# The second gate's logits of the first three units: from transposes and products on TensorE to multiply-and-sum passes on VectorE

## The chip, the core and the metric

The kernel runs on one core of a Trainium2 chip. A core has five engines that run side by side, each through its own list of instructions in order: TensorE (PE in the profile, with its weight loads as PEld), VectorE (DVE), ScalarE (ACT), GpSimd (POOL) and SyncE (SP), which here only issues DMA transfers. On-chip data lies in SBUF (128 partitions); products land in PSUM, from which VectorE or ScalarE has to take them. An engine waits at an instruction until what it needs is signalled by a semaphore, and all behind it on that engine waits too. The metric is the device time of one execution, in microseconds (us).

## What is computed

Eight batches of 256 tokens of width 128 go through two layers, each a conditioning step followed by a mixture of eight experts. Cut to the part that the change touches, the second layer is:

```python
def _L1_ffn_ref(x, gate_w, w1, b1, w2, b2, gamma, beta):
    residual = x
    mu = jnp.mean(x, axis=-1, keepdims=True)
    var = jnp.mean(jnp.square(x - mu), axis=-1, keepdims=True)
    xn = (x - mu) * jax.lax.rsqrt(var + LN_EPS) * gamma + beta
    probs = jax.nn.softmax(jnp.einsum('bld,de->ble', xn, gate_w), axis=-1)
    w, idx = jax.lax.top_k(probs, TOP_K)
    w = w / jnp.sum(w, axis=-1, keepdims=True)
    ...
    h = jax.nn.gelu(jnp.einsum('bld,edh->eblh', xn, w1) + b1[:, None, None, :], approximate=False)
    out_e = jnp.einsum('eblh,ehd->ebld', h, w2) + b2[:, None, None, :]
    output = jnp.einsum('ble,ebld->bld', cw, out_e)
    return output + residual
```

Here E is 8 experts, H 512 and TOP_K 2. The logits of the second gate are the `einsum('bld,de->ble', xn, gate_w)`: for each token the sum over 128 features of normalized x, times gamma, plus beta, times the gate's column. In the first layer every expert works on every token; in the second only the two best experts of each token do.

## The kernel before

**Tiling.** The 2048 tokens are five units: units 0, 1 and 2 have 4 tiles of 128 tokens (512), units 3 and 4 have 2 (256). `GT` is 4, so `nt == GT` picks units 0 to 2.

**The first layer** (`layer`) goes over units and, in each, over the 8 experts. For an expert, TensorE makes four hidden products (hp, L931), ScalarE takes each through the activation into hT (L933), and one expert later TensorE makes four products into an output yp (L911). VectorE multiplies yp by the gate's row (part_first, L899; that frees one of two PSUM buffers of yp) and adds it to the unit's sum (acc_first, L901). The gate rows come by a DMA of SyncE each time (gbc, L891). In float32 a product is two passes of TensorE, so a profile counts 320 for 160.

**What runs in between.** After each TensorE product `layer` calls `pump()`, which takes one step of a generator at the head of a queue, `behind`. In that queue lie, one after the other, the first layer's pooling, the search for its threshold (`threshold`, whose counting passes are L521, fl), and then, each appended when a unit's sum is ready, `adapt(u)`. So the work of a unit's `adapt` is spread between the products of the next unit, and each `adapt` begins only when the one before it has ended. A `yield` in a generator gives one product's time to the others.

**`adapt(u)`** adds the sum to x (x2T, L682; x, L686 from transposes fp, L556), runs the conditioning step (adp, L693; ha, L695; dp, L703), normalizes twice (`normed`: bn_stats L565, L566, rstd on GpSimd L572, L577), which gives zn, the first part of zr, and then makes the second gate's logits: for units 0 to 2 it transposes zn (znp, L737), takes it to SBUF with gamma and beta applied (znT, L742), multiplies by the gate on four column groups (l1q, L751), takes that down (l1s, L754), transposes it back (l1p, L758) and copies the logits to lg (L766). The short units do the same with plain products (l1p, L763). Then `top_one` picks the best expert (mx, s, ms, oh, L591 to L598), again for the second (rest, L770), th and a ScalarE tanh give the two weights (L776, L777), and sofar (L790) holds the running picks. TensorE's kp (L796, L797) counts, over tokens, how many picks of each expert came before; from it VectorE makes each token's row (pos, L816), and GpSimd scatters the tokens to DRAM (xs, L818), 8 scatters for a unit of 512. For units 2, 3 and 4 VectorE then writes the list of the tiles that are full (L638 to L674, `tiles_of`, `cumulated`, `listed`).

**The second layer** goes over 36 and a few more tiles of 128 rows: SyncE fetches the rows and the expert's weights by register offsets (L962, L970), VectorE multiplies the expert's row of b2all by the token's weight (b, L1003), TensorE transposes the rows (xtp, L991), VectorE takes them down with gamma and beta (xc, L993), then come hidden products (hps, L1006), activations (hs, L1008), output products (yps, L1015) and yt (L1019). The first three tiles are begun inside the first layer's last unit. The table b2all (128 partitions, 8 x 128) is loaded once, at the start, from a DRAM copy of b2 (L616, L619).

**The order** of each engine's list is fixed when the program is built; only the beginning and the ending are put in order by hand, in between a scheduler places the instructions, and they may stand in another order than in the source. `CHAIN_GAP`, 5, is the number of steps that `adapt` of a long unit lets pass between zn and its transposes.

Of the kernel before, what the change touches and what calls it, by code (L numbers as in the profile page):

```python
# [10 lines left out]
F32 = mybir.dt.float32  # L11
# [47 lines left out]
CHAIN_GAP = 5  # L59
# [10 lines left out]
C_G1 = C_G0 + E  # L70
# [4 lines left out]
C_LG = C_B21 + E  # L75
C_LB = C_LG + 1
# [12 lines left out]
def tile_adaln_ffn_d2(ctx: ExitStack, tc: tile.TileContext, x, ptype, lang, cols, b1v,  # L89
                      w10, w20, w11d, w21d, lw1, lw2, lgb, out):  # L90
    nc = tc.nc
# [419 lines left out]
    def threshold():  # L511
        lflat = logit.rearrange("p e t -> p (e t)")

        def below(values, name):

            n = values.shape[1]
            c = small.tile([P, 3], BF16, tag="kc", name=f"kc_{name}")
            for i in range(n):
                flags = small.tile([P, P], BF16, tag="flags", name=f"fl_{name}_{i}", bufs=2)
                with nc.allow_low_precision("counts up to 128, which bf16 holds exactly"):  # L520
                    nc.vector.tensor_scalar(flags, lflat, values[:, i:i + 1], None, ALU.is_lt, ALU.add,  # L521
                                            accum_out=c[:, i:i + 1])
            tot = pss.tile([P, 3], F32, tag="sm", name=f"kt_{name}")
            nc.tensor.matmul(tot[:, :n], lhsT=one16, rhs=c[:, :n], start=True, stop=True)  # L524
            return tot[:, :n]

        tot = below(steps.bitcast(F32)[:, SEARCH, 0:1], "s")
        found = small.tile([P, 1], I32, tag="found", name="found_s")
        nc.vector.tensor_scalar(found, tot, float(KTH), -1.0, ALU.is_gt, ALU.mult)
        for k, low in enumerate((*range(29, 0, -2), 0)):  # L530

            n = 3 if low else 1
            trial = small.tile([P, 3], I32, tag="tr", name=f"tr_{low}")[:, :n]
            nc.vector.tensor_scalar(trial, steps[:, k, :n], found, None, ALU.bitwise_xor)
            for _ in range(SEARCH_GAP if k else 0):
                yield
            tot = below(trial.bitcast(F32), str(low))
            ok = small.tile([P, 3], F32, tag="ok", name=f"ok_{low}")[:, :n]
            up = small.tile([P, 1], F32, tag="up", name=f"up_{low}")
            nc.vector.tensor_scalar(ok, tot, float(KTH), None, ALU.is_le, ALU.add, accum_out=up)  # L540
            bits = small.tile([P, 1], I32, tag="bits", name=f"bits_{low}")
            nc.vector.tensor_scalar(bits, up, float(1 << low), None, ALU.mult)
            after = small.tile([P, 1], I32, tag="found", name=f"found_{low}")
            nc.vector.tensor_tensor(after, found, bits, ALU.bitwise_xor)
            found = after
        gate = const.tile([P, P], F32, name="gate")
        nc.vector.scalar_tensor_tensor(gate, lflat, found.bitcast(F32), lflat, ALU.is_ge, ALU.mult)
        yield
        yield
        gd0[0] = rows_to_dram(gate, P, "L0")  # L550
# [57 lines left out]
    holding = const.tile([P, E], F32, name="holding")  # L608

    b2d = dram.tile([E, P], F32, name="b2d")  # L610
    b2all = const.tile([P, E, D], F32, name="b2all")
    w21 = const.tile([P, E, HC * D], F32, name="w21")


# [1 line left out]
    nc.sync.dma_start(out=b2d, in_=b2r)  # L616
    for e in range(E):
        nc.sync.dma_start(out=w21[:, e, :], in_=w21d[e].rearrange("p c d -> p (c d)"))
    nc.sync.dma_start(out=b2all.rearrange("p e d -> p (e d)"),  # L619
                      in_=b2d.rearrange("e d -> (e d)").partition_broadcast(P))  # L620
    for n in range(EARLY, B):
        nc.sync.dma_start(out=ys[n * 4 * P:(n + 1) * 4 * P, :].rearrange("(p t) d -> p t d", t=GT), in_=empty[:, :, :D])
    rows = xs.rearrange("(p m t) c -> p m (t c)", p=P, t=GT)
# [53 lines left out]
    def adapt(u, acc):  # L677
        g, o, nt = UNITS[u]
# [51 lines left out]
            nc.scalar.copy(zr[1][:, :, :D], zn)  # L730
        for s in range(2):
            nc.gpsimd.tensor_copy(zr[s].bitcast(I32)[:, :, D], dest[:, s, t0:t0 + nt])
        for _ in range(CHAIN_GAP if nt == GT else not last_unit):
            yield
        zp = psb.tile([P, GT, P], F32, tag="big", name=f"znp{u}")[:, :nt, :]
        for t in range(nt):
            nc.tensor.transpose(zp[:, t, :], zn[:, t, :], ident)  # L737
        if nt == GT:
            zt = keep.tile([P, GN], F32, tag="poolT", name=f"znT{u}")
        else:  # L740
            zt = work.tile([P, n], F32, tag="znT", name=f"znT{u}", bufs=1)
        nc.vector.tensor_scalar(zt, zp.rearrange("p t d -> p (t d)"), col[:, C_LG:C_LG + 1],  # L742
                                col[:, C_LB:C_LB + 1], ALU.mult, ALU.add)
        yield
        if not last_unit:
            yield
        if nt == GT:

            lq = pss.tile([P, P], F32, tag="sm", name=f"l1q{u}")
            for t in range(nt):  # L750
                nc.tensor.matmul(lq[t * A:(t + 1) * A, :], lhsT=col[:, C_G1:C_G1 + A], rhs=zt[:, t * P:(t + 1) * P],  # L751
                                 start=True, stop=True)
            ls = work.tile([P, P], F32, tag="gT", name=f"l1s{u}")
            nc.vector.tensor_copy(ls, lq)  # L754
            yield
            yield
            lp = pss.tile([P, GT, A], F32, tag="sm", name=f"l1p{u}")
            nc.tensor.transpose(lp.rearrange("p t c -> p (t c)"), ls, ident)  # L758
            lp = lp[:, :, :E]
        else:  # L760
# [4 lines left out]
        lg = small.tile([P, GT, E], F32, tag="ex", name=f"lg{u}")[:, :nt, :]  # L765
        nc.vector.tensor_copy(lg, lp)  # L766
# [92 lines left out]
    def run(key, steps):  # L859
        yield from steps  # L860
        done.add(key)
# [136 lines left out]
    def hidden(k, xt, wt, xc):  # L998
        hp = psb.tile([P, HC, P], F32, tag="big", name=f"hps{k}")
        hT = work.tile([P, HC, P], F32, tag="scr", name=f"hs{k}", bufs=NSCR)  # L1000

        b2 = work.tile([P, GN], F32, tag="gbc", name=f"b2_{k}", bufs=4)[:, :D]
        nc.vector.tensor_tensor(b2, b2all[:, bass.ds(number(k, DVE), 1), :].rearrange("p o d -> p (o d)"),  # L1003
                                xt[:, D + 1:D + 2].to_broadcast([P, D]), ALU.mult)
        for c in range(HC):
            nc.tensor.matmul(hp[:, c, :], lhsT=wt[:, c * P:(c + 1) * P], rhs=xc, start=True, stop=True)  # L1006
        for c in range(HC):
            nc.scalar.activation(hT[:, c, :], hp[:, c, :], AF.Gelu, bias=b1all[:, bass.ds(number(k, ACT), 1), c])  # L1008
        return k, xt, hT, b2
# [93 lines left out]
    def early():  # L1103
        for k in range(LEAD + PRIMED):
            ahead(k)
        for _ in range(PRIMED):
            flipped.append(turn(*fetched.popleft()))

    behind.append(run("poolings", poolings()))
    behind.append(run("threshold", threshold()))  # L1110
    layer("first", AF.Gelu_apprx_tanh, poolT, w10s, w20s, C_B10, C_B20, gates0, "pool", adapt,
          early)

# [101 lines left out]
```

## Time and profile before

| what | us |
|---|---|
| median of 5 runs | 354.61 (354.21 to 356.51) |
| profiled execution: its time | 357.72 |
| profiled execution: span from the first to the last instruction | 356.0 |
| TensorE's granted clock, mean, of full speed | 0.985 |
| first layer's products L931 and L911, busy | 119.9 and 119.6 |
| VectorE, all second-gate operations to be removed (L742, L754, L766 of three units) | 2.4, 0.9, 0.6 |
| weight load or product kp waiting for sofar, five times | 3.5 |

The profile is one execution, taken by the hardware's profiler. The span is divided among engines, which overlap, so busy times don't add up to it. A group's row gives the count, the busy time and the mean length of one instruction in ns, then the idle time of the engine just before and what ended it. VectorE's instructions overlap at their ends, so that two of them may start closer together than one is long. An operation with a sum beside its output shows as two rows, the operation and DVE_READ_ACCUMULATOR.

### The profile page before, as it was taken

How to read it: one execution, taken by the hardware profiler on the slowest of the kernel's cores; microseconds unless marked ns; L12 is line 12 of the kernel's file. 1: busy time of each engine (PE TensorE's matmuls, PEld its weight loads, DVE VectorE, ACT ScalarE, POOL GpSimd, SP SyncE). 2: the span in 40 equal slices, each digit the busy share in tenths (PEclk: the TensorE clock that was granted, in tenths of full speed). 3: DMA queues.
4: the chain of work that ended last, by engine and by line, in shares of the span. 5: the costliest groups of instructions: out<-in, count | busy, mean ns of one | idle time of the engine just before them, and what ended most of it. 6: DMA issues, size and time to landing. Idle time of an engine off the chain costs nothing. (4 is left out here: it accounts for less than half of the span.)

```text
span 356.0 us, 6113 instructions
## 1 busy us (share of the span) xinstructions
PE 338.8 (95%) x1668; PEld 223.4 (63%) x1668; DVE 201.0 (56%) x839; ACT 157.9 (44%) x359; POOL 93.6 (26%) x146
## 2 busy tenths in 40 slices
PE   6999999999999999999999999999999995999991
PEld 5794444444444444444444578877878995999990
DVE  2685666543144774765631267496697785345761
ACT  3476345534443335433344235443536643555620
POOL 6500000000000040452052013046143745555510
PEclk9899999999999999999999999999999999899998
DMA  5792599935223202121011012112756761677273
GB/s 169 232 343 77 146 354 381 380 135 166 74 70 111 62 29 59 52 69 29 30 63 56 15 31 37 40 45 75 193 173 191 187 175 45 158 216 222 89 253 113
DMA packets 35787, 47.56 MB, mean 134 GB/s; under 512 B 5465, under 2 KB 18604, under 8 KB 35752
## 3 DMA queue, kind: packets, MB, share of 16 engines
q1 hardware_dynamic: 32888, 42.31, 39.9%
q0 software_dynamic: 2144, 4.19, 3.4%
q10 hardware_dynamic: 720, 0.66, 0.5%
q8 instruction: 15, 0.25, 0.3%
q14 instruction: 20, 0.16, 0.2%
HBM read 32.66 MB, written 14.66 MB: 133 GB/s over the span
## 5 line engine op out<-in xcount | busy, mean ns | idle before, releaser
L933 ACT ACTIVATE hT_first<-hp_first,col 128x512 f32<-128x512 f32 (+1 forms) x160 | 92.8, 602 | 92.4 <-PE hp_first L931 82.9
L931 PE MATMUL hp_first<-poolT,w 128*128 128x512 f32 (+1 forms) x320 | 119.9, 512 | 0.6 <-ACT hT_first L933 0.6
L911 PE MATMUL yp_first<-hT_first,w 128*128 128x512 f32 (+1 forms) x320 | 119.6, 512 | 0.0
L911 PEld LDWEIGHTS yp_first<-hT_first,w 128*128 128x128 f32 x320 | 58.8, 190 | 45.3 <-issue 41.0
L931 PEld LDWEIGHTS hp_first<-poolT,w 128*128 128x128 f32 x320 | 58.5, 190 | 45.5 <-issue 40.2
L1008 ACT ACTIVATE hs<-hps,col 128x128 f32<-128x128 f32 x144 | 40.8, 369 | 38.1 <-PE hps L1006 21.5
L818 POOL DMA_INDIRECT xs<-zr,pos x32 | 31.9, 998 | 66.7 <-DVE pos L816 31.2
L1015 PE MATMUL yps<-w,hs 128*128 x288 | 38.7, 279 | 3.3 <-ACT hs L1008 3.1
L899 DVE SCALAR_TENSOR_TENSOR part_first<-yp_first,col,gbc_first 128x512 f32<-128x512 f32 (+1 forms) x28 | 17.2, 614 | 42.1 <-PE yp_first L911 40.9
L1022 POOL DMA_INDIRECT ys<-yt,xt x32 | 32.5, 1017 | 31.2 <-DVE yt L1019 24.4
L1006 PE MATMUL hps<-xc,wt 128*128 128x128 f32 x288 | 39.1, 280 | 0.5 <-issue 0.5
L1015 PEld LDWEIGHTS yps<-w,hs 128*128 128x128 f32 x288 | 35.6, 195 | 4.2 <-issue 4.2
L1006 PEld LDWEIGHTS hps<-xc,wt 128*128 128x128 f32 x288 | 35.9, 196 | 0.3 <-issue 0.2
L1019 DVE SCALAR_TENSOR_TENSOR yt<-yps,xt,b 128x128 f32<-128x128 f32 x36 | 12.5, 348 | 22.5 <-PE yps L1015 13.9
L572 POOL TENSOR_TENSOR rstd_l<-ve_l,nhalf 128x4 f32<-128x4 f32 (+1 forms) x5 | 5.2, 1040 | 68.2 <-DVE ve_l L570 67.5
L901 DVE TENSOR_TENSOR acc_first<-acc_first,part_first 128x512 f32<-128x512 f32 (+1 forms) x35 | 20.1, 580 | 0.5
L506 POOL DMA_DIRECT2D gd_L<-gT_L x1 | 0.7, 660 | 63.3 <-DVE gT_L L504 63.3
L919 ACT ACTIVATE y_first<-yp_first,col 128x512 f32<-128x512 f32 x8 | 5.5, 687 | 23.2 <-PE yp_first L911 14.6
L993 DVE TENSOR_SCALAR xc<-xtp,col 128x128 f32<-128x128 f32 x36 | 14.3, 401 | 0.0
L521 DVE TENSOR_SCALAR_CACHE_REDUCE fl<-logit,tr 128x128 bf16<-128x128 f32 x46 | 13.5, 343 | 0.6
L1003 DVE TENSOR_TENSOR b<-b2all,xt 128x128 f32<-128x128 f32 x36 | 10.2, 287 | 5.8 <-DMA xt<-xs 1.7
L540 DVE TENSOR_SCALAR_CACHE_REDUCE ok<-kt 128x3 f32<-128x3 f32 (+1 forms) x16 | 2.6, 160 | 13.8 <-PE kt L524 13.8
(241 smaller groups left out, 296.8 us busy)
## 6 DMA issues: line engine op xcount, KB each, us to landing
wt<-in_w_dram SPq DMA_DIRECT2D x36, 256.0 KB
xs<-empty SPq DMA_DIRECT2D x1, 8580.0 KB
w<-in_w_dram SPq DMA_DIRECT2D x24, 256.0 KB
gbc_first<-gd_L SPq DMA_DIRECT2D x24, 256.0 KB
xt<-xs SPq DMA_DIRECT2D x36, 65.0 KB
gbc_first<-gd_L SPq DMA_DIRECT2D x16, 128.0 KB
yg<-ys SPq DMA_DIRECT2D x8, 256.0 KB
xg<-in_x_dram SPq DMA_DIRECT2D x8, 128.0 KB
```

The lines of the kernel that those rows point to most:

```text
L521: nc.vector.tensor_scalar(flags, lflat, values[:, i:i + 1], None, ALU.is_lt, ALU.add, accum_out=c[:, i:i + 1])
L818: move = nc.gpsimd.indirect_dma_start(out=xs, out_offset=bass.IndirectOffsetOnAxis(ap=pos[:, t:t + 1], axis=0), in_=zr[s][:, t, :], in_off ...
L899: nc.vector.scalar_tensor_tensor(part, y, bias, gbc, ALU.add, ALU.mult)
L901: nc.vector.tensor_tensor(accs[u], accs[u], part, ALU.add)
L911: nc.tensor.matmul(yp, lhsT=w2s[e][:, c, :], rhs=hT[:, c, :], start=(c == 0), stop=(c == HC - 1))
L931: nc.tensor.matmul(hp, lhsT=w1s[e][:, c * P:(c + 1) * P], rhs=sources[g][:, o * P:o * P + n], start=True, stop=True)
L933: nc.scalar.activation(hT[:, c, :], hp, act, bias=col[:, cb1 + e * HC + c:cb1 + e * HC + c + 1])
L993: nc.vector.tensor_scalar(xc, tp, col[:, C_LG:C_LG + 1], col[:, C_LB:C_LB + 1], ALU.mult, ALU.add)
L1006: nc.tensor.matmul(hp[:, c, :], lhsT=wt[:, c * P:(c + 1) * P], rhs=xc, start=True, stop=True)
L1008: nc.scalar.activation(hT[:, c, :], hp[:, c, :], AF.Gelu, bias=b1all[:, bass.ds(number(k, ACT), 1), c])
L1015: nc.tensor.matmul(yp, lhsT=hT[:, c, :], rhs=w21[:, bass.ds(ek, 1), c * D:(c + 1) * D], start=(c == 0), stop=(c == HC - 1))
L1022: move = nc.gpsimd.indirect_dma_start(out=ys, out_offset=bass.IndirectOffsetOnAxis(ap=xt.bitcast(I32)[:, D:D + 1], axis=0), in_=yt, in_off ...
```

## The change

For units 0 to 2 the logits come from VectorE alone. A new generator, `second_gate`, stands in `behind` after `threshold`: it scales the identity by gamma (scale), multiplies the gate by it on TensorE, so that g1p holds the 8 x 128 table gamma times gate, and beside it, in a 129th column, beta times gate; it copies the table to SBUF (g1r), writes it to DRAM (g1d) and loads it back to all partitions (g1all, 128 x 8 x 129). `adapt` then makes, for each of 8 experts and 4 tiles, one `scalar_tensor_tensor` with constant 1, zn times the table's row, whose sum over the 128 features goes into lg: 32 passes for a unit, 96 in all, with a `yield` after every third; one addition then puts in the beta column. The transposes, products and copies of these units (L737, L742, L751, L754, L758, L766) are gone, and so is their gap of `CHAIN_GAP` steps: from zn to the logits there were 9 yields, now there are 11. The tables g1all and b2all share one buffer (`tag="eight"`, `bufs=1`), so b2all is now loaded after unit 2's logits, on SyncE's queue, where it has to wait until the last of them has read g1all. Units 3 and 4 stay as they were.

```diff
-    b2all = const.tile([P, E, D], F32, name="b2all")
+    g1d = dram.tile([E, D + 1], F32, name="g1d")
+    eights = {}
+
+    def eight(name, rows, width):
+
+        eights[name] = const.tile([P, E, D + 1], F32, tag="eight", name=f"{name}all", bufs=1)[:, :, :width]
+        nc.sync.dma_start(out=eights[name].rearrange("p e d -> p (e d)") if width > D else eights[name],
+                          in_=rows.rearrange("e d -> (e d)").partition_broadcast(P) if width > D else
+                          rows.partition_broadcast(P))
+
+    def second_gate():
+        scale = work.tile([P, P], F32, tag="gT", name="scale")
+        nc.vector.tensor_scalar(scale, ident, col[:, C_LG:C_LG + 1], None, ALU.mult)
+        yield
+        yield
+        g1p = pss.tile([E, D + 1], F32, tag="sm", name="g1p")
+        nc.tensor.matmul(g1p[:, :D], lhsT=col[:, C_G1:C_G1 + E], rhs=scale, start=True, stop=True)
+        nc.tensor.matmul(g1p[:, D:], lhsT=col[:, C_G1:C_G1 + E], rhs=col[:, C_LB:C_LB + 1], start=True, stop=True)
+        g1r = const.tile([E, D + 1], F32, name="g1r")
+        nc.vector.tensor_copy(g1r, g1p)
+        nc.sync.dma_start(out=g1d, in_=g1r)
+        eight("g1", g1d, D + 1)
...
-    nc.sync.dma_start(out=b2all.rearrange("p e d -> p (e d)"),
-                      in_=b2d.rearrange("e d -> (e d)").partition_broadcast(P))
...
-        for _ in range(CHAIN_GAP if nt == GT else not last_unit):
+        lg = small.tile([P, GT, E], F32, tag="ex", name=f"lg{u}")[:, :nt, :]
+        if nt == GT:
+
+            g1 = eights["g1"]
+            for n, (e, t) in enumerate(itertools.product(range(E), range(nt))):
+                spent = small.tile([P, D], F32, tag="spent", name=f"spent{u}_{n}", bufs=2)
+                nc.vector.scalar_tensor_tensor(spent, zn[:, t, :], 1.0, g1[:, e, :D], ALU.mult, ALU.mult,
+                                               accum_out=lg[:, t, e:e + 1])
+                if n % 3 == 2:
+                    yield
+            nc.vector.tensor_tensor(lg, lg, g1[:, :, D].unsqueeze(1).to_broadcast([P, nt, E]), ALU.add)
+            if u == NU - 3:
+                eight("b2", b2d, D)
             yield
...
-        if nt == GT:
-
-            lq = pss.tile([P, P], F32, tag="sm", name=f"l1q{u}")
-            for t in range(nt):
-                nc.tensor.matmul(lq[t * A:(t + 1) * A, :], lhsT=col[:, C_G1:C_G1 + A], rhs=zt[:, t * P:(t + 1) * P],
-                                 start=True, stop=True)
-            ls = work.tile([P, P], F32, tag="gT", name=f"l1s{u}")
-            nc.vector.tensor_copy(ls, lq)
-            yield
-            yield
-            lp = pss.tile([P, GT, A], F32, tag="sm", name=f"l1p{u}")
-            nc.tensor.transpose(lp.rearrange("p t c -> p (t c)"), ls, ident)
-            lp = lp[:, :, :E]
...
-        nc.vector.tensor_tensor(b2, b2all[:, bass.ds(number(k, DVE), 1), :].rearrange("p o d -> p (o d)"),
+        nc.vector.tensor_tensor(b2, eights["b2"][:, bass.ds(number(k, DVE), 1), :].rearrange("p o d -> p (o d)"),
...
     behind.append(run("threshold", threshold()))
+    behind.append(run("gate", second_gate()))
```

More of the change, by code (lines that the diff above doesn't have):

```diff
@@ L732, in adapt @@
             nc.gpsimd.tensor_copy(zr[s].bitcast(I32)[:, :, D], dest[:, s, t0:t0 + nt])
-        for _ in range(CHAIN_GAP if nt == GT else not last_unit):
-            yield
-        zp = psb.tile([P, GT, P], F32, tag="big", name=f"znp{u}")[:, :nt, :]
-        for t in range(nt):
-            nc.tensor.transpose(zp[:, t, :], zn[:, t, :], ident)
-        if nt == GT:
-            zt = keep.tile([P, GN], F32, tag="poolT", name=f"znT{u}")
-        else:
+        lg = small.tile([P, GT, E], F32, tag="ex", name=f"lg{u}")[:, :nt, :]
@@ new lines, in adapt @@
+        if nt == GT:
[9 more added lines that the diff above has]
+                eight("b2", b2d, D)
+            yield
+        else:
+            for _ in range(not last_unit):
+                yield
+            zp = psb.tile([P, GT, P], F32, tag="big", name=f"znp{u}")[:, :nt, :]
+            for t in range(nt):
+                nc.tensor.transpose(zp[:, t, :], zn[:, t, :], ident)
@@ L741, in adapt @@
             zt = work.tile([P, n], F32, tag="znT", name=f"znT{u}", bufs=1)
-        nc.vector.tensor_scalar(zt, zp.rearrange("p t d -> p (t d)"), col[:, C_LG:C_LG + 1],
-                                col[:, C_LB:C_LB + 1], ALU.mult, ALU.add)
-        yield
-        if not last_unit:
+            nc.vector.tensor_scalar(zt, zp.rearrange("p t d -> p (t d)"), col[:, C_LG:C_LG + 1],
+                                    col[:, C_LB:C_LB + 1], ALU.mult, ALU.add)
             yield
-        if nt == GT:
-            lq = pss.tile([P, P], F32, tag="sm", name=f"l1q{u}")
-            for t in range(nt):
-                nc.tensor.matmul(lq[t * A:(t + 1) * A, :], lhsT=col[:, C_G1:C_G1 + A], rhs=zt[:, t * P:(t + 1) * P],
-                                 start=True, stop=True)
-            ls = work.tile([P, P], F32, tag="gT", name=f"l1s{u}")
-            nc.vector.tensor_copy(ls, lq)
-            yield
-            yield
-            lp = pss.tile([P, GT, A], F32, tag="sm", name=f"l1p{u}")
-            nc.tensor.transpose(lp.rearrange("p t c -> p (t c)"), ls, ident)
-            lp = lp[:, :, :E]
-        else:
+            if not last_unit:
+                yield
@@ L764, in adapt @@
                                  start=True, stop=True)
-        lg = small.tile([P, GT, E], F32, tag="ex", name=f"lg{u}")[:, :nt, :]
-        nc.vector.tensor_copy(lg, lp)
+            nc.vector.tensor_copy(lg, lp)
         oh1, l1 = top_one(lg, f"p{u}")
```

## The prediction

> **What bounds the kernel now.** First the busy time by engine, then the same by stage, then TensorE's instructions in order of time around the removed ones. The chain of waits is of no use here: it stops after its last piece, a ScalarE copy of 0.36 us.
>
> ```profile
> PE 338.8 (95%) x1668; PEld 223.4 (63%) x1668; DVE 201.0 (56%) x839; ACT 157.9 (44%) x359; POOL 93.6 (26%) x146
> ```
>
> ```profile
> core 0: us, PE busy (x) PEld busy (x) DVE busy (x) ACT busy (x) POOL busy (x), PEclk, DMA share, GB/s
> 118.00:148.00 30.00, 29.66 (x94) 13.12 (x93) 19.75 (x73) 10.44 (x17) 5.17 (x6) 1.00 0.16 40
> 205.00:235.00 30.00, 29.94 (x154) 24.50 (x154) 19.87 (x82) 13.68 (x33) 3.77 (x5) 1.00 0.15 36
> ```
>
> These two stretches hold the routing of units 0 and 2. TensorE is busy 29.7 and 29.9 of 30 us, VectorE 19.8: TensorE's list sets the pace, and what is taken from it, or makes it wait, moves the end. VectorE has 10 us free in 30, but not at every moment.
>
> ```profile
> 137.04 0.60 PE L737 MATMUL znp<-ident,zr 128*128 128x128 f32 x4
> 137.48 1.02 PE L911 MATMUL yp_first<-hT_first,w 128*128 128x512 f32 x2
> 138.34 1.02 PE L931 MATMUL hp_first<-poolT,w 128*128 128x512 f32 x2
> 139.29 0.42 PE L751 MATMUL l1q<-znT,col 128*32 128x128 f32 x8
> 139.65 1.98 PE L931 MATMUL hp_first<-poolT,w 128*128 128x512 f32 x4
> 141.47 0.27 PE L758 MATMUL l1p<-ident,l1s 128*128 128x128 f32 x1
> 141.58 1.02 PE L931 MATMUL hp_first<-poolT,w 128*128 128x512 f32 x2
> 142.44 2.74 PE L911 MATMUL yp_first<-hT_first,w 128*128 128x512 f32 x6
> 145.52 0.19 PE L796 MATMUL kp<-sofar,one 128*128 128x40 bf16 x1 [0.34 <-DVE sofar L790]
> 145.58 1.10 PE L911 MATMUL yp_first<-hT_first,w 128*128 128x512 f32 x2
> ```
>
> Columns: start, length, engine, line, operation. The reader sees three removed pieces (znp, l1q, l1p) between expert products, and kp, which stays, and for which TensorE stands still until VectorE has finished sofar.
>
> **What is removed from TensorE.** An expert's four products of 512 columns (8 passes) start 3.43 us apart from the next ones (127.60, 131.04, 134.47), 0.429 a pass. znp costs 137.48 - 137.04 = 0.44. l1q: 138.34 plus two passes is 139.20, work goes on at 139.65: 0.45. l1p: 139.65 plus four passes is 141.37, on at 141.58: 0.21. Together 1.10; the same sums give 1.09 in unit 1 (znp at 169.16) and 1.10 in unit 2 (224.68). **Removed: 3.3.** Added once: g1p, two passes of 128 columns (0.11 each, as znp) and two of one column (l1p of the short units takes 0.37 for four narrow ones): **0.4**. Net -2.9.
>
> **What a pass on VectorE costs.** No row has this operation with a sum and two sources, so it comes from neighbours.
>
> ```profile
> 56.02 0.35 DVE L521 TENSOR_SCALAR_CACHE_REDUCE fl<-logit,tr 128x128 bf16<-128x128 f32 x1
> 56.29 0.09 DVE L521 DVE_READ_ACCUMULATOR fl<-logit,tr 128x1 bf16 x1
> 56.29 0.34 DVE L521 TENSOR_SCALAR_CACHE_REDUCE fl<-logit,tr 128x128 bf16<-128x128 f32 x1
> 56.55 0.09 DVE L521 DVE_READ_ACCUMULATOR fl<-logit,tr 128x1 bf16 x1
> ```
>
> ```profile
> L899 DVE SCALAR_TENSOR_TENSOR part_first<-yp_first,col,gbc_first 128x512 f32<-128x512 f32 x14 | 10.5, 750 | 35.6 <-PE yp_first L911 35.5
> L686 DVE TENSOR_TENSOR x<-fp,xg 128x512 f32<-128x512 f32 x3 | 2.1, 691 | 2.3 <-PE hp_first L931 1.7 <-PE fp L556 0.6
> L547 DVE SCALAR_TENSOR_TENSOR gate<-logit,found 128x128 f32<-128x128 f32 x1 | 0.4, 353 | 0.0
> ```
>
> ```profile
> L593 DVE TENSOR_TENSOR s_p<-lg,mx_p x5: 174/191/193, 142.2 to 285.0; 128x32 f32<-128x32 f32 x3, 128x16 f32<-128x16 f32 x2
> L770 DVE SCALAR_TENSOR_TENSOR rest<-oh_p,lg x5: 165/191/193, 143.1 to 286.4; 128x32 f32<-128x32 f32 x3, 128x16 f32<-128x16 f32 x2
> ```
>
> The threshold's counting passes (fl, 128x128 with a sum, a scalar from a column) follow each other every 0.265 us, the reading of the sum inside that. A column scalar costs 0.059 (L899 less L686); a constant costs nothing (L770 as L593), and the new passes have the constant 1. So 0.265 - 0.059 = 0.207. As a check: two tensor operations of 256 (L716) start 0.334 apart; less 128 elements at 1.06 ns ((688 - 417)/256, L901) leaves 0.198. Bounds: 0.20 below; above, gate's 353 ns with an unhidden 86 ns reading, 0.44. I take 0.207, as both neighbours agree.
>
> [...]
>
> VectorE gains 96 x 0.207 = 19.9 and loses 3 x (0.81 + 0.28 + 0.19) = 3.8. What matters is whether sofar comes in time for kp, behind which all expert products stand. Where an operation stands in each engine's list is read from the order of the two built programs; a "pair" is part_first and acc_first of one expert (0.78 + 0.69, or 0.93 for 256 columns), which stand among the passes.
>
> **Unit 0.** zr starts at 131.86 in both kernels, and the next operation at 132.89. In the new list come 32 passes (6.62) with one part/acc pair among them (1.5): logits at 141.0. The table's bias add 0.13, then the chain from mx to sofar, 142.00 to 145.46 = 3.46, with the next pair inside (about 1.25): 145.8. kp now stands after the first product of the next unit's expert 1: 134.47 + 3 x 3.43 + 0.86 = 145.6. **Wait 0.2.**
>
> **Unit 1.** Counted from the start of expert 1's hidden products (146.52 before): dp stands 1.4 further back in the list (8.7 for 7.3), so zr comes 18.3 after, not 16.9. Add 1.04 for zr, 1.5 + 1.5 for two pairs, 6.62, 0.25, 3.46: sofar at 32.7. kp's place, after expert 5's hidden products: 4 x 6.86 + 3.43 + 2.04 (the adapter's products) = 32.9. **No wait.**
>
> **Unit 2** runs beside 256-column products, 1.73 a group. 220.35 + 6.62 + two pairs 1.86 + 0.25 + 4.05 (229.67 to 233.72, a pair inside) = 233.1; kp's place 222.96 + 6 x 1.73 = 233.3. **No wait.** Here an output buffer is freed late too: expert 5's pair ends near 230.4, needed by expert 7 at 231.6.
>
> kp cost TensorE 0.56, 0.57 and 0.29 before (the passes around it), 1.42; now 0.2 each (as kp of unit 4, at 288.39), and 0.2 of wait: 0.8. **-0.6.** ScalarE's tanh (th) waits for VectorE too, with the next activations behind it; it is due 1.8 before sofar (143.68 for 145.46), and its activations feed products of the next expert, so it costs nothing unless VectorE is later than kp can bear anyway.
>
> **What moves.** The routing takes two steps more, so unit 3's adapter and routing come one expert later: kp3 from before expert 7's hidden products to the first of expert 6's outputs. One of the first b operations now stands before sofar is done; kp3 would wait about 0.8 (0.2 before). After it VectorE has some 18 operations (list of tiles, one pair), near 3.9 us, before the first xc, and TensorE has 1.3 + 0.2 + 1.7 until it needs that: 0.6 for 0.37 before. **+0.9**, at nothing to 2.5.
> On SyncE's queue the b2 load moves from 44.40 behind the gate rows of unit 4's expert 0. It waits for the table's last reading, near 228, and is issued near 236; a 256 KB gate load took 3.1 from issue (81.37) to use (84.50), so 512 KB are an estimated 6, before the first use at 260.8: 18 of cover; without it up to 6. Gate loads queue behind it, but VectorE reaches them later. g1's write and its 516 KB load go in among the gate loads at 81 to 89; what stands behind is first needed at 101.7, the table at 132.9. POOL's scatters follow kp, which in unit 2 keeps its time to 0.3; the first tile fetch (248.49) was 12 ahead of its transpose (262.28).
>
> **Sum.** -2.9 - 0.6 + 0.9 = -2.6. The profiled span of 356.0 (357.72 with what lies around it) becomes 353.4. The median shown, 354.61, becomes **352.0**.
>
> **Rivals.**
> *VectorE late (slower).* Each pass longer by d makes each of three waits longer by 32 d. With x = 32 d the waits are 0.2 + x, x - 0.2 and x - 0.2: the added cost is 3x - 0.4 once x passes 0.2. It eats the gain at x = 1.0 (a pass of 0.238) and makes the kernel 0.5% slower from x = 1.6 (0.257). If fl's 0.265 holds as it stands, x = 1.86, +5.2: 357.2. At gate's 353 plus 86 ns, x = 7.4: 374. For it: that row 0.265, and that no row has this form. Against: the column scalar's 0.059. Chance 0.30, for passes from 0.257 on.
> *Given back at the boundary (no change).* kp3 and the first tiles wait 2.5 rather than 0.9, and unit 0 waits up to 1 more: 353.6 to 354.6. For it: VectorE is busy for 20.1 of 27 us from 235 to 262 and takes work of unit 3 into the next stretch. Against: TensorE was idle there for less than 1 us, so the lists fit. Chance 0.15.
> *TensorE's gain doesn't reach the end*, as ScalarE or a transfer sets it: at 297.3 all engines stand still for 3.1 us until ScalarE goes on, with no cause that the trace names. If that instant is fixed: 354.6. Chance 0.05.
> Forecast: 0.50.
>
> **How the numbers follow.** The forecast's own range: no wait before kp and no cost at the boundary, -3.7, to the 0.5% below, -1.8: 350.9 to 352.8. 0.5%, 1.8 us, is about what a measurement of this kernel can tell from no change. With the others the range is **350.5 to 358.5**; above it lies a pass of 0.28 or more, 0.13, below it 0.04. Faster by more: 0.50, the forecast. Within it: 0.20, the second and third rival. Slower: 0.30, the first.
>
> **What would show it.** In the profile after: znp, l1q and l1p of three units gone from TensorE; 96 passes, each with a reading of the sum, every 0.20 to 0.22 us; TensorE's idle time before kp released by sofar, under 1 us in all; kp3 and the first hps waiting about 1.4 together; b2all landed before 250. The prediction is wrong if passes start more than 0.24 apart: then TensorE waits before kp three times, by 32 times the excess each.

## The result, and the profile after

The changed kernel took 356.9 us (353.77 to 361.82), the kernel before 355.35 (353.49 to 362.58) beside it: a ratio of **1.0034, with a 95% interval of 1.0018 to 1.005**. The ratio goes by the executions within 1.5% of the fastest of their kernel, which leaves out 7 of the 36 and 4 of the 62 that the ranges include. That is within the 0.5% that the prediction called no change, but its interval lies above 1: a little slower, where 352.0, faster, had been forecast. The profiled execution has a span of 356.2, before 356.0.

First the busy time by engine of the changed kernel's page, then the same two stretches as before.

```profile
PE 335.6 (94%) x1633; PEld 222.2 (62%) x1633; DVE 218.5 (61%) x1027; ACT 158.1 (44%) x359; POOL 93.6 (26%) x146
```

```profile
core 0: us, PE busy (x) PEld busy (x) DVE busy (x) ACT busy (x) POOL busy (x), PEclk, DMA share, GB/s
118.00:148.00 30.00, 29.93 (x83) 13.21 (x82) 25.17 (x132) 11.42 (x19) 4.05 (x5) 1.00 0.13 42
205.00:235.00 30.00, 29.36 (x143) 24.80 (x143) 25.16 (x145) 14.28 (x34) 3.78 (x5) 1.00 0.20 52
```

TensorE lost 3.2 us of work (338.8 to 335.6), and the span lost nothing: the 3.2 us became idle time. VectorE went from 19.8 to 25.2 in each stretch. In the first one TensorE is as full as it was, in the second it has begun to wait.

VectorE's instructions in order of time, in unit 0: start, length, engine, line, operation.

```profile
133.21 0.28 DVE L759 SCALAR_TENSOR_TENSOR spent<-zr,g1all 128x128 f32<-128x128 f32 x1
133.43 0.08 DVE L759 DVE_READ_ACCUMULATOR spent<-zr,g1all 128x1 f32 x1
133.43 0.28 DVE L759 SCALAR_TENSOR_TENSOR spent<-zr,g1all 128x128 f32<-128x128 f32 x1
133.64 0.08 DVE L759 DVE_READ_ACCUMULATOR spent<-zr,g1all 128x1 f32 x1
```

A pass starts every 0.2125 us; the reading of its sum lies inside. The prediction had 0.207. TensorE's list beside them (the view of the first two rows ends at 140):

```profile
134.79 3.60 PE L928 MATMUL yp_first<-hT_first,w 128*128 128x512 f32 x8
138.22 2.31 PE L948 MATMUL hp_first<-poolT,w 128*128 128x512 f32 x5
...
141.66 3.60 PE L928 MATMUL yp_first<-hT_first,w 128*128 128x512 f32 x8
145.09 1.02 PE L948 MATMUL hp_first<-poolT,w 128*128 128x512 f32 x2
146.18 0.18 PE L813 MATMUL kp<-sofar,one 128*128 128x40 bf16 x1
```

Groups of four products follow one another every 3.43 with nothing in between: znp, l1q and l1p are gone. Two passes from 145.09 would end at 145.95; kp starts at 146.18, a wait of 0.2, as forecast. The gain is really made here. Next, where it goes: all waits of TensorE over 0.5 us between unit 1's routing and unit 4's adapter, with what stands on the releasing engine. (kp0 to kp3 and dp3 are kp and dp of that unit.)

```profile
179.39 0.18 PE L813 MATMUL kp<-sofar,one 128*128 128x40 bf16 x1 [0.84 <-DVE sofar L807]
...
229.59 0.20 ACT L794 ACTIVATE th<-th 128x4 f32<-128x4 f32 x1 [2.96 <-DVE th L793]
230.21 0.70 PE L948 MATMUL hp_first<-poolT,w 128*128 128x256 f32 x2 [0.64 <-ACT hT_first L950]
...
240.37 0.49 PE L723 MATMUL dp<-lw,ha 33*128 33x128 f32 x4
240.79 1.13 PE L948 MATMUL hp_first<-poolT,w 128*128 128x256 f32 x4
242.18 0.29 DVE L728 TENSOR_TENSOR xr<-dp,x 128x128 f32<-128x128 f32 x1 [0.78 <-PE hp_first L948]
242.53 0.70 PE L948 MATMUL hp_first<-poolT,w 128*128 128x256 f32 x2 [0.61 <-issue]
243.65 0.47 ACT L950 ACTIVATE hT_first<-hp_first,col 128x256 f32<-128x256 f32 x1 [4.96 <-PE hp_first L948]
244.18 0.70 PE L948 MATMUL hp_first<-poolT,w 128*128 128x256 f32 x2 [0.95 <-issue]
...
258.94 0.16 DVE L807 TENSOR_TENSOR sofar<-sofar,sel 128x8 bf16<-128x8 bf16 x1
260.18 0.29 DVE L1020 TENSOR_TENSOR b<-b2all,xt 128x128 f32<-128x128 f32 x1 [1.08 <-issue]
260.39 0.15 DVE L807 TENSOR_TENSOR sofar<-sofar,sel 128x8 bf16<-128x8 bf16 x1
260.60 0.17 PE L813 MATMUL kp<-sofar,one 128*128 128x24 bf16 x1 [0.77 <-DVE sofar L807]
268.60 0.33 PE L1008 MATMUL xtp<-ident,xt 128*128 128x128 f32 x1 [1.32 <-DVE xc L1010]
```

Read from the top: VectorE is late for unit 1's sofar; ScalarE stands idle for 2.96 us until VectorE has made th, and TensorE then waits for an activation; behind dp3, hidden products wait in two steps, as VectorE and ScalarE take up dp3 and the first of those products 1.3 to 2.8 us after TensorE made them; a b operation between the two halves of sofar holds up kp3; and the third tile's xc is late. Together 5.1 us. Before, the same stretch had these three, 1.2 together:

```profile
177.62 0.19 PE L796 MATMUL kp<-sofar,one 128*128 128x40 bf16 x1 [0.33 <-DVE sofar L790]
247.77 1.56 PE L931 MATMUL hp_first<-poolT,w 128*128 128x256 f32 x6 [0.64 <-ACT hT_first L933]
264.60 0.33 PE L991 MATMUL xtp<-ident,xt 128*128 128x128 f32 x1 [0.20 <-issue]
```

The operation b takes 0.29 itself; VectorE stands idle for 1.08 just ahead of it. In that time lies the load of the expert's number into a register, which the kernel asks for there (L998): the trace has it on VectorE's queue from 259.0, 0.97 long, and b starts at 260.18. In the run without passes (below), which loads b2all at the start, the idle time ahead of the first b is 1.01, so that the late table doesn't make it.

The first columns of these rows also give a measure that can be compared from run to run. It takes the start of unit 0's fp, of unit 2's fp, and of the first of the late transposes at the end (first in the changed kernel, then in the kernel before):

```profile
119.03 0.60 PE L556 MATMUL fp<-ident,acc_first 128*128 128x128 f32 x4
203.58 0.66 PE L556 MATMUL fp<-ident,acc_first 128*128 128x128 f32 x4
343.23 1.06 PE L1098 MATMUL late<-yt,home 128*128 128x128 f32 x8
```

```profile
118.70 0.60 PE L556 MATMUL fp<-ident,acc_first 128*128 128x128 f32 x4
205.35 0.63 PE L556 MATMUL fp<-ident,acc_first 128*128 128x128 f32 x4
342.10 1.06 PE L1081 MATMUL late<-yt,home 128*128 128x128 f32 x8
```

The **first stretch** is 203.58 - 119.03 = 84.55 (routing of units 0 and 1), the **second** 343.23 - 203.58 = 139.65 (units 2 to 4 and the tiles). Before: 86.65 and 136.75. The gain of 2.1 in the first is followed by a loss of 2.9 in the second. What lies ahead of the first stretch and behind the second varies from one execution to another, by up to 3 us ahead (116.87 to 120.01 in the changed kernel's profiles), so that the stretches say more than the spans.

### The profile page after: what moved, and what is told of

Read it like the earlier page. It is cut to its first block, busy times and chain, and to the rows that moved or that the text cites. A ratio compares the mean times of both kernels' runs of the same rounds, so it can differ in the third digit from the quotient of the medians.

```text
span 356.2 us, 6231 instructions
## 1 busy us (share of the span) xinstructions
PE 335.6 (94%) x1633; PEld 222.2 (62%) x1633; DVE 218.5 (61%) x1027; ACT 158.1 (44%) x359; POOL 93.6 (26%) x146
## 5 line engine op out<-in xcount | busy, mean ns | idle before, releaser
L759 DVE SCALAR_TENSOR_TENSOR spent<-zr,g1all 128x128 f32<-128x128 f32 x96 | 21.2, 283 | 0.0
L918 DVE TENSOR_TENSOR acc_first<-acc_first,part_first 128x512 f32<-128x512 f32 (+1 forms) x35 | 20.1, 580 | 0.4
```

The lines of the kernel that those rows point to most:

```text
L759: nc.vector.scalar_tensor_tensor(spent, zn[:, t, :], 1.0, g1[:, e, :D], ALU.mult, ALU.mult, accum_out=lg[:, t, e:e + 1])
L918: nc.vector.tensor_tensor(accs[u], accs[u], part, ALU.add)
```

## The experiments

They ran in five sets, each set on a chip of its own and with its own runs of the kernel before. That kernel took 355.4 beside the result, 347.9, 348.3 and 347.1 in the first three sets, and 356.3 and 355.7 in the last two. I call them **quiet sets** (348) and **full sets** (355). As no chip came twice among them, the record can't tell whether a level goes with the chip or with the time of the set. Ratios are to the kernel before of the same set, with the 95% interval.

| kernel | first | second | ratio |
|---|---|---|---|
| quiet: before | 86.67 | 129.61 | 1 |
| changed | 84.59, 84.53 | 130.00, 129.95 | 0.9976 (0.9952 to 1.0), 0.9952 (0.9926 to 0.9979) |
| passes in units 0 and 1 | 84.54 | 129.73 | 0.9946 (0.9924 to 0.9968) |
| the same, 13 steps | 83.34 | 129.63 | 0.9924 (0.9897 to 0.9951) |
| passes in unit 2 alone | 86.66 | 129.45 | 1.001 (0.9979 to 1.0042) |
| no passes, 11 steps in unit 2 | 86.67 | 131.85 | 1.0091 (1.0057 to 1.0125) |
| changed, 9 steps in unit 2 | 84.55 | 131.22 | 1.0008 (0.9983 to 1.0034) |
| changed, 9 steps in all | 86.81 | 131.10 | 1.0067 (1.0039 to 1.0096) |
| 9 steps in unit 2, b after sofar | 84.53 | 131.11 | 0.9998 (0.9974 to 1.0021) |
| changed, th behind kp | 84.55 | 129.70 | 0.9973 (0.9942 to 1.0003) |
| 13, 13, 11 steps, th behind kp | 83.34 | 129.79 | 0.9926 (0.9896 to 0.9957) |
| full: before | 86.65, 86.67 | 136.75, 136.78 | 1 |
| changed | 84.55 | 139.65 | 1.0034 (1.0018 to 1.005), 1.0048 (1.0008 to 1.0087) |
| passes in units 0 and 1, 13 steps | 83.34 | 136.88 | 0.9908 (0.9869 to 0.9947) |
| no passes, 11 steps in unit 2 | 86.66 | 139.81 | 1.0094 (1.0057 to 1.0131) |
| changed, 9 steps in unit 2 | 84.55 | 140.68 | 1.003 (0.9998 to 1.0063) |
| 13, 13, 11 steps, th behind kp | 83.33 | 139.95 | 0.9931 (0.9901 to 0.9961) |

Two executions of one kernel agree in the first stretch to 0.06. The stretches are of one profiled execution, the ratios of all. The row of the changed kernel in the full sets has one profile for two ratios: the other is of an execution of 362.92, where the median is 357.17, with stretches of 84.53 and 143.97.

### Is it the place of unit 3's work, or the passes?

Unit 2 with 9 steps and not 11, all passes kept:

```diff
-                if n % 3 == 2:
+                if n % (4 if u == 2 else 3) == (3 if u == 2 else 2):
```

> The changed kernel, but in unit 2 a yield after every fourth pass and not after every third: 9 steps from zn to the logits, as before the change. Unit 3's adapter then stands where it stood before (dp3 ahead of output products, kp3 ahead of expert 7's hidden products). Theory A, the two steps: in the changed kernel's trace TensorE was 3.7 us ahead at 239 us and lost 3.9 us between 240 and 269, because unit 3's adapter and routing stood elsewhere; with the old place the loss goes, while kp2 comes one or two steps earlier and may wait about 0.5: 2.5 to 3.5 us less than the changed kernel's, a ratio to the kernel before of 0.990 to 0.996. Theory B, VectorE's load: the 32 passes of unit 2 make VectorE late for unit 3 wherever that stands: 1.003 or more. Theory C, the late load of b2all: it stays late here: 1.003.

And the place without a pass, in the kernel before:

```diff
-        for _ in range(CHAIN_GAP if nt == GT else not last_unit):
+        for _ in range(CHAIN_GAP + 2 * (u == 2) if nt == GT else not last_unit):
```

> The kernel before, without a single pass, with 7 in place of 5 empty steps in unit 2 alone: unit 3's adapter and routing stand where the changed kernel has them (dp3 right ahead of hidden products). Theory A: the loss at the boundary comes without any pass: 2 to 4 us slower than before, 1.006 to 1.011, with TensorE standing still between dp3 and expert 4's products and before the third tile. Theory B: VectorE has no more work than before: 0.999 to 1.002. Theory C: b2all is loaded at the start: 0.999 to 1.002.

The second run lost 0.9% without a pass: its second stretch grew from 129.61 to 131.85. So the two steps alone cost 2.2 us. But the first run did not win them back: 131.22. Theory A is right that the place costs, and wrong that it is all: passes in the old place cost 1.6, the place without passes 2.2, and both together only 0.4. In the run with 9 steps TensorE waited 0.65 for hT, 0.33 before kp2, 0.33 before the second half of dp3 and this long before kp3 (TensorE's row, and VectorE's in front of it):

```profile
254.60 0.29 DVE L1020 TENSOR_TENSOR b<-b2all,xt 128x128 f32<-128x128 f32 x1 [0.99 <-DMA wt<-in_w_dram]
255.65 0.36 DVE L807 TENSOR_TENSOR sofar<-sofar,sel 128x8 bf16<-128x8 bf16 x2
256.06 0.17 PE L813 MATMUL kp<-sofar,one 128*128 128x24 bf16 x1 [1.28 <-DVE sofar L807]
```

All three units with `n % 4 == 3`:

> The changed kernel with a yield after every fourth pass in all three units: 9 steps from zn to the logits everywhere. Theory A: the boundary is as in the run with unit 2 alone, but kp of units 0 and 1 stands two steps (1.7 us) earlier, while sofar comes when VectorE has done its passes, so that kp0 waits about 1.9 and kp1 about 2.5 us where the changed kernel had 0.2 and 0.8: some 3 us slower than the run with unit 2 alone, a ratio of 0.999 to 1.005. If VectorE's order lets the passes come earlier too, the ratio is that of the run with unit 2 alone. Theories B and C: 1.003 or more.

1.0067, and kp0 waited 1.80, kp1 1.35 (forecast: 1.9 and 2.5):

```profile
146.03 0.18 PE L813 MATMUL kp<-sofar,one 128*128 128x40 bf16 x1 [1.80 <-DVE sofar L807]
```

That is the price of VectorE being late, with the same passes and two steps fewer in each unit: the first stretch went from 84.55 to 86.81. The steps move kp, and all behind it with it.

### Which units bring the gain?

The old way for unit 2 (`if u in (0, 1):` ahead of the passes; the other branch is the code before), with the table b2all still loaded late; and its complement, passes for unit 2 alone.

> Passes for units 0 and 1 alone; unit 2 goes the old way over TensorE with its 9 steps; the table g1all stays, and b2all is loaded late as in the changed kernel. Theory A: two units' gain without the loss: in the changed kernel's trace TensorE was 2.6 us ahead when unit 1's routing was over (at 195 us): 0.991 to 0.995. Theory B says the same. Theory C: b2all comes late all the same, and the loss stays: 1.000 to 1.004.

> The complement: passes for unit 2 alone, in 11 steps; units 0 and 1 go the old way over TensorE. If the gain is made in units 0 and 1 (2.1 us by the traces) and unit 2's passes take 1.1 us off TensorE only to wait as long before hT, kp3 and the tiles: 0.3 to 0.6 more than before, 1.000 to 1.003 (with g1p's 0.4). If the loss in the changed kernel came from having all three together, for the late tables or for VectorE's total load: 0.996 to 0.998, a third of the gain.

0.9946 and 1.001. Units 0 and 1 bring all of it, 2.1 us. Unit 2's passes take 1.1 off TensorE and bring nothing: 129.45 for 129.61, with g1p on top. As the late b2all is in the faster one, theory C falls; a run of a full set with it, further down (0.9908), says the same.

Then, with passes in units 0 and 1 alone, two more empty steps behind them:

```diff
...
+            for _ in range(2):
+                yield
             nc.vector.tensor_tensor(lg, lg, g1[:, :, D].unsqueeze(1).to_broadcast([P, nt, E]), ALU.add)
```

> Passes for units 0 and 1 alone, and two more empty steps after their passes (13 from zn to the logits), so that kp0 and kp1 stand 1.7 us later. If the waits before kp0 (0.2) and kp1 (0.8) come from VectorE's passes ending late, they go: about 1.0 less than with 11 steps (0.9946): 0.990 to 0.993. If the later scatters or the later end of the routing of units 0 and 1 matter, 0.994 or more.

0.9924, the first stretch 83.34, and no wait before kp0 or kp1 in the trace. It holds in a full set too, 0.9908. **It beats both kernels in either kind of set.**

### Can unit 2's waits be taken away?

The first two b operations tied behind unit 3's last sofar, in the version with 9 steps:

> Passes in all three units, 9 steps in unit 2, and the first two b operations tied to come after the last of unit 3's sofar on VectorE, where the kernel before has them. In the run with 9 steps TensorE waited 1.28 before kp3, for sofar, and a b operation with 0.99 of idle time ahead of it stood between th and sofar. If that b is what made kp3 late: no wait over 0.3 there and 0.8 to 1.2 us less, a ratio of 0.997 to 0.998. If VectorE is late for unit 3 anyhow: kp3 still waits over 0.8, and the ratio stays at 1.0008.

```profile
256.73 0.17 PE L816 MATMUL kp<-sofar,one 128*128 128x24 bf16 x1 [0.17 <-DVE sofar L809]
263.87 0.33 PE L1011 MATMUL xtp<-ident,xt 128*128 128x128 f32 x1 [1.01 <-DVE xc L1013]
```

b, with the idle time ahead of it, did make kp3 late: 1.28 became 0.17. But 1.01 before the third tile took its place, and the second stretch stayed at 131.1; 0.8 to 1.2 less had been expected. Moving th behind kp in the changed kernel went the same way:

```diff
-        nc.scalar.activation(th, th, AF.Tanh, scale=0.5)
+        if u != 2:
+            nc.scalar.activation(th, th, AF.Tanh, scale=0.5)
...
+        if u == 2:
+            move = nc.scalar.activation(th, th, AF.Tanh, scale=0.5)
+            tc.add_manual_dep(move.ins, counted.ins.name, SYNC, reason="no activation waits for it")
```

> The changed kernel with one thing moved: in unit 2, ScalarE's tanh (th) is tied to come after kp's products and so stands behind the activations of expert 0 of the next unit, not ahead of expert 7's last one. In the changed kernel ScalarE stood idle for 2.97 us until VectorE had made th, and TensorE then 0.66 for hT, while kp2 itself did not wait; my prediction had put this at nothing. If th is the cause: no wait for hT near 228, and, as the kernels' lists show, the first b operations come after sofar again: TensorE's waits before hT and kp3 (0.66 and 0.77) shrink, and the stretch from unit 2's fp to unit 4's last transposes is 0.8 to 1.4 shorter than the changed kernel's 130.0: a ratio 0.002 to 0.004 below the changed kernel's in this set. If VectorE's lateness for unit 2 has to be paid anyhow, at kp2 or behind it, the stretch stays at 130.0 and the ratio is the changed kernel's.

The waits for hT and kp3 (0.66 and 0.77) are both gone, and 1.06 before a tile's transpose is new; 130.0 became 129.70, and the ratio is no lower than the changed kernel's in that set (0.9973 and 0.9952). In these two runs VectorE is behind at this point, and the repair hands the wait on to the next taker. The steps of units 0 and 1 and th behind kp together:

> Passes in all three units, with what the other runs found put together: two more steps for units 0 and 1 (13), 11 for unit 2, and th of unit 2 behind kp. Expected: units 0 and 1 as in the run with 13 steps (83.3 from unit 0's fp to unit 2's, for 86.7 before and 84.6 changed), and from there on 128.6 to 129.6 for 129.6 to 130.0: a ratio of 0.989 to 0.993, as fast as passes for units 0 and 1 alone (0.9924) or faster. If unit 2's passes cost more than they bring even so: 0.993 to 0.996.

0.9926: what units 0 and 1 bring, and nothing from unit 2.

### Why is the changed kernel slower in one set and faster in another?

Two repeats of the changed kernel and two of the kernel before:

> The changed kernel as it is, beside the others of this set, for a profile on the same chip. Theory A (two steps of unit 2 move unit 3's work, and unit 2's passes are late for what waits on them): the ratio found before, 1.002 to 1.005, with TensorE waiting before kp1 (0.8), for hT in unit 2's routing (0.6), before kp3 (0.8) and before the third tile (1.0 to 1.3). The idle pair between dp3 and expert 4's products (0.6 and 0.95) and the standstill of 3.8 us near 297 are either part of the kernel and come again, or belong to the one execution shown: the same list of unit 3 without passes had neither.

> The changed kernel a third time, beside the others of this set, as its two ratios (1.0034 and 0.9976) exclude each other. If the difference lay in the executions of the first set, which had the standstill near 297: 0.996 to 1.000 again. If the sets differ at random by some 0.3%: anywhere from 0.997 to 1.004.

> The kernel before as it is, for a profile beside the others. If the standstill of 3.1 us near 297 and the slower clock after it belong to the execution shown, they are absent here, as in the four runs of the first set, and the span is some 7 us shorter than 356.0. From unit 0's fp to the last transposes: 230.6 then; about 223 expected here.

> The kernel before, for a second profile: from unit 0's fp to the first late transposes 216.3 and from unit 0's fp to unit 2's 86.7, as in the other one, if nothing stands still; 223 with the standstill.

In the quiet sets the changed kernel is 0.2 to 0.5% faster (the interval of the first reaches 1.0), where the first repeat had been expected slower, as in the result. Its stretches are 84.6 and 130.0; before, 86.67 and 129.61: a gain of 1.7 in sum. Two windows show what a full set has and a quiet one lacks; first the changed kernel of the result, then the same kernel in a quiet set, whose times are 2 us earlier:

```profile
238.00:248.00 10.00, 8.45 (x41) 6.24 (x41) 7.11 (x37) 3.14 (x9) 6.34 (x7) 1.00 0.26 74
296.00:302.00 6.00, 2.23 (x17) 2.07 (x17) 1.87 (x9) 1.27 (x6) 3.60 (x4) 0.94 0.14 45
```

```profile
238.00:248.00 10.00, 10.00 (x49) 8.48 (x48) 6.85 (x35) 5.14 (x12) 6.30 (x9) 1.00 0.31 88
296.00:302.00 6.00, 5.66 (x51) 5.47 (x49) 2.50 (x9) 2.85 (x11) 4.48 (x5) 1.00 0.82 249
```

In the quiet set there is no standing behind dp3, no standstill near 297, and no wait over 0.15 before the third tile. The second profile of the kernel before has the standstill in a full set (3.75, second stretch 136.78), and the first repeat has none in a quiet one (129.61). So the standstill belongs to the set, not to the change. The change costs more where it is: in a full set the second stretch grows by 2.9, in a quiet one by 0.4.

> The changed kernel once more, beside the best version. Three sets gave 1.0034, 0.9976 and 0.9952; only the first set's executions stood still for 3 to 4 us near 297 and took 355 rather than 348. If this set's runs of before are near 348: 0.995 to 0.998 again, with no standstill. If they are near 355: 1.002 to 1.005, and the standstill is in the profile.

> Passes for units 0 and 1 with 13 steps, once more, beside the changed kernel. If units 0 and 1 bring the gain and unit 2's passes bring none: 0.990 to 0.994 whichever the set, as its own work from unit 2 on is that of before; 0.002 to 0.005 below the changed kernel where that is undisturbed, 0.009 to 0.012 below where it is disturbed. If the disturbance falls on whatever is changed: 1.000 or more in a disturbed set.

1.0048 and 0.9908, in a full set: with unit 2 as before, the second stretch is 136.88 for 136.78. The loss goes with what is changed in unit 2.

> The kernel before, no passes, with two more empty steps in unit 2: unit 3's list as in the changed kernel. In sets whose kernel before takes 355 to 356, the changed kernel stood still 1.6 to 3.0 between dp3 and expert 4's products, which the kernel before never does. If the order of unit 3's work makes that stand, it comes here too, without a pass, in such a set: 1.006 to 1.014. If it takes the passes: 1.004 to 1.008, what the two steps cost elsewhere (1.8 to 2.2 by the traces), and no standing behind dp3. In a set near 348: 1.005 to 1.009.

> All passes, but 9 steps in unit 2 and so the order of before for unit 3. In a set near 355 to 356: no standing behind dp3 if the order makes it (the ratio 0.998 to 1.002, below the changed kernel's 1.0034 to 1.0048), and 1.003 or more with such a standing if the passes make it. In a set near 348: 1.000 as before (1.0008).

> All passes, 13 steps for units 0 and 1, 11 for unit 2, and th of unit 2 behind kp. In a set near 355 to 356: if unit 3's order meets the disturbance here as in the changed kernel, 0.995 to 1.000, worse than passes for units 0 and 1 alone (0.9908); if not, 0.989 to 0.994. In a set near 348: 0.9926 as before.

1.0094, 1.003 and 0.9931; second stretches of 139.81, 140.68 and 139.95. The place alone costs 3.0 in a full set, the passes alone 3.9, both 2.9. So neither the order of unit 3's work nor the passes make the loss by themselves: each loses about 3 us there. Nor is it the standing behind dp3, which took 1.56 in the result and 2.32 in the other profile, but 0.54 without passes and 0.15 in the last run, and with 9 steps came as 0.73 and 0.23 at dp3 itself.

The last run doesn't fit. Its stretches say -3.3 + 3.2, about nothing; its ratio says -2.5, within what had been expected if the order meets no disturbance. Its profile is of the slowest of its 12 executions (355.84, median 353.62). For the other four versions of the full sets, stretches and ratio agree to 0.8 us. So by time the last run lost nearer 1 than 3 in its second stretch, and th behind kp may help in a full set after all; no set has it beside the changed kernel, so that this isn't shown. In the version without a pass, TensorE waited at these points, among others:

```profile
243.78 0.70 PE L931 MATMUL hp_first<-poolT,w 128*128 128x256 f32 x2 [0.54 <-ACT hT_first L933]
264.18 0.33 PE L991 MATMUL xtp<-ident,xt 128*128 128x128 f32 x1 [1.00 <-DVE xc L993]
268.28 0.33 PE L991 MATMUL xtp<-ident,xt 128*128 128x128 f32 x1 [1.50 <-DVE xc L993]
```

Why VectorE and ScalarE take up TensorE's results so late in a full set, and why the same lists lose more there, stays **open**: the trace names no releaser, and no run took it away.

## Why the prediction was wrong

The prediction summed to -2.6. By its steps:

- **TensorE's work**, -2.9: right, 338.8 to 335.6 (-3.2). **A pass**, 0.207: right, 0.2125. The new rows, two sources with a sum, take 0.28 each, where gate's, two sources without one, took 0.35; they start 0.2125 apart, near the lower bound of 0.20 and far from the upper one of 0.44. The rival "VectorE late" had a longer pass as its condition, and falls with it, although VectorE is late.
- **Unit 0**, a wait of 0.2: right. **Unit 1**, "No wait": wrong, 0.84 in the result, 0.81 to 0.85 in the quiet sets. I followed VectorE's list and TensorE's, not GpSimd's. These rows are of the changed kernel, GpSimd and VectorE:

```profile
149.08 1.13 POOL L835 DMA_INDIRECT xs<-zr,pos  x1 [16.66 <-ACT hT_first L950]
...
158.13 0.96 POOL L835 DMA_INDIRECT xs<-zr,pos  x1 [0.30 <-issue]
159.12 1.05 POOL L572 TENSOR_TENSOR rstd_l<-ve_l,nhalf 128x4 f32<-128x4 f32 x1
160.20 1.11 DVE L577 TENSOR_SCALAR xr<-xr,mv_l,rstd_l 128x128 f32<-128x128 f32 x4 [2.90 <-POOL rstd_l L572]
```

  and before:

```profile
146.71 1.13 POOL L818 DMA_INDIRECT xs<-zr,pos  x1 [14.61 <-DVE pos L816]
158.47 1.11 DVE L577 TENSOR_SCALAR xr<-xr,mv_l,rstd_l 128x128 f32<-128x128 f32 x4 [1.17 <-POOL rstd_l L572]
```

  Unit 0's eight scatters start at 149.08, 2.4 later than before (146.71), as kp came later and a pair of part_first and acc_first stood ahead of pos. Unit 1's rstd_l stands behind them on GpSimd and starts at 159.12, not 157.40; VectorE waits 2.90 for it and not 1.17. zr starts at 165.17, 20.1 after expert 1's hidden products, where I had counted 18.3. The run with 13 steps took the wait away (83.34); it did not move the scatters, so that this is their doing is read from the trace, not shown by a run.
- **Unit 2**, "No wait": right for kp2. Wrong in the sentence that the tanh "costs nothing unless VectorE is later than kp can bear anyway": VectorE was in time for kp2, and ScalarE still stood 2.96 us for th with an activation behind it that TensorE needed at once: 0.64. The run with th behind kp shows that.
- **What moves**, +0.9: the step that failed. kp3's wait was 0.77 as priced (0.8), and b did stand before sofar. But I priced one wait and one tile: the third tile's was 1.32 in the result, not 0.6. And I put nothing for the products behind dp3, which now stands right ahead of hidden products and no longer ahead of output products: they waited 1.56 in the result. In the quiet sets the same lists have neither wait, so that a size read from the lists can't have been right for both. Without any pass this place cost 2.2 (quiet) and 3.0 (full). In place of unit 2's -1.1, its share of kp and the +0.9, together about -0.3, the second stretch was +0.4 in the quiet sets and +2.9 in the result. That was most of the error; unit 1's wait of 0.84 was the rest (2.1 gained in the first stretch, where the terms make 2.7).
- **b2all and the other transfers**, nothing: right in effect; b2all was issued at 227.22, not near 236, and the version that loads it late is the fastest.

In a quiet set this makes -2.1 + 0.4 = -1.7, in the result -2.1 + 2.9 = +0.8; the ratios make -0.8 and -1.7 in the quiet sets, +1.2 in the result. g1p's 0.4 lies ahead of unit 0's fp, where executions differ by more. The rival "Given back at the boundary" is nearest to what happened in the result, with kp3 and the first tiles, and behind dp3 besides; it stopped at no change. I gave it 0.15 against 0.50, as TensorE was idle there for less than 1 us before. That said that the lists fitted, not by how much.

## What to carry to other kernels

Work taken off the bounding engine is worth what the next taker can bear, unit by unit: the same 32 passes brought 1.05 us a unit in units 0 and 1, taken together (1.67 with two steps more), and nothing in unit 2. There VectorE had its list of tiles to make and short products beside it, which is the likely reason; no run took these away. When work moves to another engine, follow every queue that its result passes through to the next unit (here GpSimd's scatters and ScalarE's tanh), and try the change for each unit alone. When steps are added between work of two units, look at which kind of product the next unit's work now stands in front of.

## What the runs showed that I had not expected

- The kernel before has two levels, 347 to 348 and 355 to 356, by set. Some 7 us of the difference lie in the second stretch (129.6 and 136.8): a standstill of 3.1 to 3.8 near 297, TensorE's granted clock near half for 3.4 us after it (0.50 from 302 to 304 in the profile before), and smaller waits near 247.
- The change's sign depends on that level: 0.9952 and 0.9976 at the lower, 1.0034 and 1.0048 at the upper. What changed unit 2's or unit 3's work cost up to 2.2 us of the second stretch at the lower (the changed kernel 0.4, unit 2's passes alone nothing) and 2.9 to 3.9 at the upper (for one version less by its time than by its profile), where nothing on TensorE's list says so.
- Effects did not add up, in the quiet sets: two steps +2.2, passes in unit 2 with the old steps +1.6, both +0.4.
